# A graph layer's setup, reordered: the first two groups' picks beside the key table, the rest of the table in later steps

## The chip, the cores and the metric

The kernel runs on one core of a Trainium2 chip. A core has five engines that run their own instruction queues in order: TensorE (PE, matrix products into PSUM), VectorE (DVE), ScalarE (ACT), GpSimd (POOL) and SyncE (SP), which here only issues DMAs. The metric is the device time of one execution in microseconds (us). Times of the kernel before: a median of 1493.0 us over three runs, 1492.52 to 1494.01.

## The reference

A message-passing layer with 6250 nodes of 64 features and 200000 edges sorted by target node, followed by a residual and a normalisation:

```
w   = silu(edge_attr_32 @ W1 + b1) @ W2 + b2            # (E, 9)
msg = einsum('ef,em,fmg->eg', x[src], edge_attr_9 * w, W_tp)
agg = segment_sum(msg, dst) / sqrt(16)
gamma, beta = split(silu(node_vec[:, None] @ Wn1 + bn1) @ Wn2 + bn2, 2)
out = layernorm(x + agg * (1 + gamma) + beta)
```

## The kernel before, in words

**Groups and steps.** The edges are cut into tiles of 128 and these into 98 groups of 16 tiles (`KB`). `setup` prepares constants and the first groups; then a loop of 98 steps runs, and step i finishes the window products of group i, the weights of group i + 1 and the first layer of group i + 2.

**Rows of x.** Each tile needs the 128 rows `x[src]`. They come in three ways. Most tiles are gathered by an indirect DMA that POOL issues (L99, one a tile), up to `AHEAD` = 6 groups ahead, into seven buffers `hs`; a buffer comes free after the window product (L533) of its group. The last `picked(g)` tiles of a group, four, or three in every fifth group, are not gathered but picked by TensorE (`pick`, L488): a tile's one-hot matrix `hot_k` (seven blocks, `hots`, L481, on VectorE) is multiplied by all of x, which stands in SBUF as a high and a low part (`xs`, 14 matmuls of 448 columns, L500) and VectorE selects one of seven columns per row and adds up (L509, L511). In every fourth group from 7 on, one tile's rows are loaded one by one by SP (L115, 32 in a step).

**The key table.** `hots` compares a key per edge. `keys_of` (L204, ten VectorE operations) makes from `src` a key and a remainder `jl` for each picked edge. `keys_first` (L225) spreads the keys of groups 0 and 1 with a diagonal (L232) and a product with ones (L233). For all other groups `keys_rest` (L235) transposes the key table in three blocks (L239), copies them on ScalarE (L241) and stores them to the DRAM table `kd`; `load_keys` (L414) reads it back to all partitions as `kr`, and `keys` (L476) copies it to PSUM for each group.

**Weights and windows.** `hidden` (L424) and `second` (L442) are the two layers of the edge network. `weights` (L452) turns their result and multiplies it by the edge's nine coefficients and by `oh`, the one-hot of the edge's target relative to its tile's first node (`near`, L404), which needs the node differences `rel = dst - row`. `windows` (L519) sums the rows by target in PSUM, `project` applies W_tp, `place` and `bring` put windows at their nodes, `finish` normalises.

**Setup's order.** The order in the text is the order on each engine (a manual schedule). `split` (L245) makes the high and low part of x, one seventh at a time, as ScalarE copies and VectorE subtracts. Then come the picks of group 0, both layers, the whole remaining key table (L277), the transposes of small tables (`p_row`, `p_f`, `p_cn`, `p_nid`), all differences `rel` (L327, 1536 columns), and the loop with step 0, in which group 1 is picked. PSUM tags that matter: `px` has two buffers (picks), `s` one (`second`, and in setup pk of group 1), `r` one (keys), `pz` two (windows), `p1` one. `SPG` are the groups with rows by SP.

Of the kernel before, what the change touches and what calls it, by code (L numbers as in the profile page):

```python
# [7 lines left out]
F32 = mybir.dt.float32  # L8
I32 = mybir.dt.int32
# [7 lines left out]
P = 128  # L17
N, F, M, D, H, E = 6250, 64, 9, 32, 64, 200000
NJ = 49
# [48 lines left out]
def gnn_resnorm_kernel(ctx: ExitStack, tc: tile.TileContext, x, src, dst, dst_row, ea, sh, cn,  # L68
# [18 lines left out]
    with ExitStack() as fast:  # L87
# [58 lines left out]

        def setup(temp):
# [12 lines left out]
            row_i = xb.rearrange("p j f -> p (j f)")[:, 0:NBLK * KB].bitcast(I32)  # L160
            load(0, split=True)
            nc.sync.dma_start(dst_i[:, 0:2 * KB], dst[:, 0:2 * KB])
            nc.sync.dma_start(row_i[:, 0:2 * KB], rows(dst[0, 0:2 * KB], P))
# [5 lines left out]
            for c in range(KB // 4):  # L169
                q = c * D  # L170
                nc.sync.dma_start(b2c[q:q + 2 * M, :], bass.AP(tensor=b2.tensor, offset=b2.offset,
                                                               ap=[[0, 2], [1, M], [1, 1]]))
            first_i = temp.tile([NBLK, KB], I32)
            nc.sync.dma_start(first_i, dst[0].rearrange("(g k) -> g k", k=KB))
            cn_j = temp.tile([NJ, P], F32)
            nc.sync.dma_start(cn_j, cn)

# [4 lines left out]
            sel_i = temp.tile([KB, P], I32)  # L182
# [5 lines left out]
            for g in range(AHEAD):  # L188
                gather(g)

# [6 lines left out]
            nc.vector.tensor_copy(li, n_i[:, 0:J])  # L197
            ones = temp.tile([P, P], F32)
            nc.vector.memset(ones, 1.0)


            zt_r = ztw

            def keys_of(g0, g1):  # L204

                c0, c1 = g0 * Q, g1 * Q
                s_f, kp, kh, rest, t0, t1 = [zt_r[:, k * C + c0:k * C + c1] for k in range(6)]
                ti = [t.bitcast(I32) for t in (t0, t1)]
                g2 = min(g1, NBLK - 1)
                nc.vector.tensor_copy(s_f[:, 0:(g2 - g0) * Q].rearrange("p (g k) -> p g k", k=Q),  # L210
                                      src_i.rearrange("p (g k) -> p g k", k=KB)[:, g0:g2, KB - Q:])
                if g1 == NBLK:
                    nc.vector.tensor_copy(s_f[:, (g2 - g0) * Q:], src_i[:, NT - Q:NT])
                nc.vector.tensor_scalar(ti[0], s_f, 2675.0, None, op0=ALU.mult)
                nc.vector.tensor_scalar(ti[0], ti[0], 17, None, op0=ALU.logical_shift_right)
                nc.vector.tensor_copy(kp, ti[0])
                nc.vector.scalar_tensor_tensor(rest, kp, -float(J * J), s_f, op0=ALU.mult, op1=ALU.add)
                nc.vector.tensor_scalar(ti[1], rest, 37.0, None, op0=ALU.mult)
                nc.vector.tensor_scalar(ti[1], ti[1], 8, None, op0=ALU.logical_shift_right)
                nc.vector.tensor_scalar(kh, ti[1], float(P), None, op0=ALU.mult)  # L220
                nc.vector.tensor_add(s_f, kp, kh)
                nc.vector.scalar_tensor_tensor(jl[:, c0:c1], kh, -float(J) / P, rest, op0=ALU.mult, op1=ALU.add)
                return s_f

            def keys_first(g, kf, tag):  # L225

                pk_t[g] = psum.tile([P, Q, P], F32, tag=tag, name=f"pk{g}")
                for t in range(picked(g)):
                    c = (g + 1) * Q - picked(g) + t
                    d0 = NBLK * KB + c * P  # L230
                    dg = xb.rearrange("p j f -> p (j f)")[:, d0:d0 + P]
                    nc.vector.tensor_scalar(dg, ident, kf[:, c:c + 1], None, op0=ALU.mult)  # L232
                    nc.tensor.matmul(pk_t[g][:, t, :], ones, dg, start=True, stop=True)  # L233

            def keys_rest(kf):  # L235
                for c0 in range(LB * Q, C, P):
                    n = min(P, C - c0)
                    p_kt = psum.tile([P, P], F32, tag="r", name=f"p_kt{c0}")
                    nc.tensor.transpose(p_kt[0:n], kf[:, c0 - LB * Q:c0 - LB * Q + n], ident)  # L239
                    kt = zt_r[:, 6 * C + c0 // 2:6 * C + c0 // 2 + P // 2].bitcast(F16)  # L240
                    nc.scalar.copy(kt[0:n], p_kt[0:n])  # L241
                    nc.sync.dma_start(kd[c0:c0 + n, :], kt[0:n])


            def split(h):  # L245
                xh = gam[:, h * J:(h + 1) * J, :].rearrange("p l f -> p f l")
                nc.scalar.copy(xs[0][:, h], xh)
                nc.vector.tensor_sub(xs[1][:, h], xh, xs[0][:, h].bitcast(F32))

            kf = keys_of(0, LB)  # L250
            keys_first(0, kf, "r")
            hots(0, 0, 1)
            for h in range(J):
                split(h)
                if h == J // 2:
                    hots(0, 1, 2)
            one = temp.tile([1, 1], F32)
            nc.vector.memset(one, 0.0)
            nc.scalar.activation(one, one, AF.Silu)
            pick(0, 0)  # L260
            hots(0, 2, Q)
            hidden(0)
            keys_first(1, kf, "s")
            hots(1, 0, 1)
            nc.vector.tensor_copy(wi, n_i[:, 0:W])
            nc.vector.tensor_sub(rel[:, 0:2 * KB], dst_i[:, 0:2 * KB], row_i[:, 0:2 * KB])
            near(0)
            pick(0, 1)
            hots(1, 1, Q)
            second(0)  # L270
            pick(0, 2, [[lambda: None, lambda: None], weights(0)])
            hidden(1)

            nc.sync.dma_start(dst_i[:, 2 * KB:], dst[:, 2 * KB:])
            nc.sync.dma_start(row_i[:, 2 * KB:], rows(dst[0, 2 * KB:], P))
            load(LB)
            keys_rest(keys_of(LB, NBLK))  # L277
            load_keys(LB)
            for q in range(2):
                n = (M + 1 - q) // 2  # L280
                nc.sync.dma_start(wtc2[q * F:(q + 1) * F, 0:n, :], wtp[:, q:M:2, :])
            nc.vector.memset(wtc2[F:P, 4], 0.0)
            zero = temp.tile([P, 1], F32)
            nc.vector.memset(zero, 0.0)
            nc.scalar.copy(zt[F:P, :, 4].rearrange("p a k w -> p a (k w)"),
                           zero[F:P, :, None].to_broadcast([F, 4, KW]))
            nc.sync.dma_start(wn1c, wn1.rearrange("o h -> h o"))
            nc.sync.dma_start(bn1c, bn1.unsqueeze(1))
            nc.sync.dma_start(wn2a[0:H, :], wn2)
            nc.sync.dma_start(wn2a[H:H + 1, :], bn2.unsqueeze(0))  # L290
            row_f = temp.tile([P, len(SPG)], F32)
            nc.vector.tensor_scalar(row_f, src_i[:, SPG[0] * KB:NBLK * KB:SPS * KB], 4.0 * F, None, op0=ALU.mult)
            p_row = psum.tile([len(SPG), P], F32, tag="s", name="p_row")
            nc.tensor.transpose(p_row, row_f, ident)
            nc.vector.tensor_copy(row_a, p_row)
            first_t = temp.tile([NBLK, KB], F32)
            nc.scalar.copy(first_t, first_i)
            p_f = psum.tile([KB, NBLK], F32, tag="s", name="p_f")
            nc.tensor.matmul(p_f, first_t, ident[0:NBLK, 0:NBLK], start=True, stop=True)
            nc.scalar.copy(first_f, p_f)  # L300
            p_cn = psum.tile([P, NJ], F32, tag="r", name="p_cn")
            nc.tensor.matmul(p_cn, cn_j, ident[0:NJ, 0:NJ], start=True, stop=True)
            cn_s = temp.tile([P, NJ], F32)
            nc.scalar.copy(cn_s, p_cn)
            nc.sync.dma_start(cn_d, cn_s)
            gate_load(0)

            nc.vector.tensor_copy(lo, lo_i)
            sel_a = temp.tile([KB, P], F32)
            nc.vector.tensor_scalar(sel_a, sel_i, -0.5, None, op0=ALU.is_gt)  # L310
            sel = temp.tile([KB, P], F32)
            nc.vector.scalar_tensor_tensor(sel, sel_i, W - 0.5, sel_a, op0=ALU.is_lt, op1=ALU.mult)
# [6 lines left out]
            p_nid = psum.tile([P, NBLK], F32, tag="s", name="p_nid")  # L319
            nc.tensor.matmul(p_nid, sel, first_f, start=True, stop=True)  # L320
            nc.vector.scalar_tensor_tensor(nid, p_nid, pw, lo, op0=ALU.add, op1=ALU.subtract)
            nc.vector.tensor_add(ident2, ident[:, 0:F], ident[:, F:P])
            for k in range(2):
                nc.vector.memset(ht[k][H:H + 1], 1.0)
            nc.vector.memset(eps, EPS)

            nc.vector.tensor_sub(rel[:, 2 * KB:], dst_i[:, 2 * KB:], row_i[:, 2 * KB:])  # L327
            nc.vector.memset(rel[:, NT:], 0.0)
            if E % P:
                nc.vector.memset(rel[E % P:, NT - 1:NT], 0.0)  # L330
# [579 lines left out]
```

## Time and profile before

| what | us |
|---|---|
| median of the timed runs | 1493.0 |
| profiled execution | 2388.1 |
| its span | 2386.3 |
| PE busy | 1675.3 (70%) |
| DVE busy | 1206.6 (51%) |
| ACT busy | 521.1 (22%) |
| POOL busy, nearly all in 1168 gathers | 1109.7 (47%) |
| L500, 5208 pick matmuls, busy | 1304.3 |
| PE's first matmul of pick(2,0) begins | 148.7 |

The profiled execution is much longer than a timed one, so its durations of single instructions are of more use than its sum. In the timeline a line gives start, duration, engine, source line, operation and, in brackets, the idle time before it and what ended that; "remote" means that no releaser was found, "issue" that the engine waited for nothing that the profile shows. Ends of matmuls are modelled.

### The profile page before, as it was taken

To read this page: it belongs to the slowest core of one execution; us is meant where nothing else is said; L and a number is where in the kernel's file an instruction comes from. 1 tells how busy PE (TensorE), PEld (TensorE's weight loads), DVE (VectorE), ACT (ScalarE), POOL (GpSimd) and SP (SyncE) were. 2 spreads that over 40 slices of the span, in tenths; PEclk is the share of its full clock that TensorE was granted. 3 is DMA by queue.
4 is the path that set the end of the run, shared out by engine and by line. 5 is a ranking of instruction groups with operands and counts; after the bars stand their busy time and mean duration, and the time that the engine had idled before them with its cause. 6 is when DMAs were issued, how large, how long until landed. Compare 5 with 4: busy or idle time off the path is not lost. (4 is left out here: it accounts for less than half of the span.)

```text
span 2386.3 us, 34188 instructions
## 1 busy us (share of the span) xinstructions
PE 1675.3 (70%) x10858; PEld 1367.1 (57%) x10858; DVE 1206.6 (51%) x2157; ACT 521.1 (22%) x1326; POOL 1109.7 (47%) x1177
## 2 busy tenths in 40 slices
PE   3076777676776767677767677677777676877797
PEld 2065656564655655556656556565656564656586
DVE  3154545454545454545555545454545454545476
ACT  1021212121212121211222222121212121212133
POOL 7644444444444545444545454545444544444410
PEclk7598888888888988887888898788887888888898
DMA  3121111111111111111111111111111111111110
GB/s 114 34 62 40 47 34 41 36 46 37 38 35 42 41 39 38 44 37 38 35 36 44 38 37 45 35 36 35 47 34 37 36 45 35 37 35 46 33 38 5
DMA packets 90264, 96.13 MB, mean 40 GB/s; under 512 B 36744, under 2 KB 51290, under 8 KB 90074
## 3 DMA queue, kind: packets, MB, share of 16 engines
q1 hardware_dynamic: 52122, 53.89, 7.9%
q0 software_dynamic: 37376, 38.35, 7.1%
q8 instruction: 89, 1.46, 0.2%
q10 hardware_dynamic: 576, 1.61, 0.2%
q14 instruction: 101, 0.83, 0.1%
HBM read 92.01 MB, written 1.73 MB: 39 GB/s over the span
## 5 line engine op out<-in xcount | busy, mean ns | idle before, releaser
L99 POOL DMA_INDIRECT hs<-in_x_dram,src_i x1168 | 1108.4, 949 | 1167.6 <-PE pz L533 825.8
L500 PE MATMUL px<-xs_w,hot_k 128*128 128x448 f32 x5208 | 1304.3, 406 | 432.3 <-DVE xm L509 377.0
L500 PEld LDWEIGHTS px<-xs_w,hot_k 128*128 128x128 f32 x5208 | 1067.0, 213 | 567.4 <-DVE xm L509 409.5
L509 DVE SCALAR_TENSOR_TENSOR xm<-li,jl,px 128x448 f32<-128x448 f32 x372 | 251.8, 677 | 936.4 <-remote 698.0
L485 DVE TENSOR_TENSOR hot_k<-pk,nk 128x896 fp32r<-128x896 f32 x372 | 387.7, 1081 | 2.8 <-PE pk L233 2.8
L511 DVE TENSOR_REDUCE hs<-xm 128x64 f32<-128x448 f32 x372 | 230.6, 620 | 12.9
L438 ACT ACTIVATE st<-p,b1c 128x1024 f32<-128x1024 f32 x98 | 109.2, 1115 | 542.4 <-PE p L429 365.3
L543 ACT COPY ztw<-pz 64x140 f32<-64x140 f32 (+1 forms) x780 | 209.2, 268 | 21.7 <-PE pz L533 10.3
L447 PE MATMUL p<-st,w2p 128*32 128x256 f32 x784 | 71.8, 430 | 152.4 <-DVE xb L370 102.9
L601 ACT COPY carry<-ps 128x128 f32<-128x128 f32 x48 | 12.8, 266 | 649.4 <-PE ps L595 587.0
L533 PEld LDWEIGHTS pz<-a,hs 128*64 128x64 f32 x3116 | 116.5, 155 | 58.7 <-issue 55.1
L447 PEld LDWEIGHTS p<-st,w2p 128*32 128x32 f32 x784 | 17.6, 113 | 228.7 <-issue 127.1
L533 PE MATMUL pz<-a,hs 128*64 128x63 f32 x3116 | 131.7, 244 | 11.7 <-issue 11.5
L467 DVE TENSOR_TENSOR a<-oh,p 128x1008 f32<-128x1008 f32 x98 | 117.9, 1203 | 3.3
L429 PE MATMUL p<-ea,w1bd 64*128 64x512 f32 x392 | 111.5, 642 | 0.7 <-issue 0.7
L728 ACT ACTIVATE var<-var,eps 128x2 f32<-128x2 f32 (+1 forms) x25 | 7.4, 295 | 374.6 <-DVE var L725 374.6
L579 PE MATMUL pt<-ztw,wtc 128*64 128x112 f32 x960 | 71.9, 308 | 18.6 <-ACT st L438 18.6
L579 PEld LDWEIGHTS pt<-ztw,wtc 128*64 128x64 f32 x960 | 61.7, 170 | 20.6 <-ACT st L438 20.3
L554 DVE TENSOR_TENSOR r<-pt,r 112x128 fp32r<-112x128 f32 x48 | 13.9, 289 | 97.2 <-issue 86.2
L479 ACT CAST pk<-kr 128x512 f32<-128x512 f16 (+1 forms) x96 | 54.6, 569 | 16.5 <-DVE hot_k L485 11.1
L450 ACT ACTIVATE p2s<-p,b2c 128x256 f32<-128x256 f32 x98 | 45.9, 468 | 48.6 <-issue 30.5
L457 DVE STREAM_TRANSPOSE p<-p2s 128x256 f32<-128x256 f32 x98 | 44.1, 450 | 14.9 <-issue 14.4
(138 smaller groups left out, 552.7 us busy)
## 6 DMA issues: line engine op xcount, KB each, us to landing
hs<-in_x_dram SPq DMA_DIRECT2D x2944, 0.2 KB
ea<-in_ea_dram SPq DMA_DIRECT2D x48, 512.0 KB
hs<-in_x_dram,src_i POOLq DMA_INDIRECT x1168
kr<-kd SPq DMA_DIRECT2D x48, 256.0 KB
sh<-in_sh_dram SPq DMA_DIRECT2D x49, 144.0 KB
cb<-cn_d SPq DMA_DIRECT2D x12, 128.0 KB
out_dram<-o SPq DMA_DIRECT2D x24, 64.0 KB
dst_i<-in_dst_dram SPq DMA_DIRECT2D x1, 768.0 KB
```

What stands on the lines that cost most here:

```text
L99: hs_dma[g] = [nc.gpsimd.indirect_dma_start(out=hs[g][:, t - g * KB, :], out_offset=None, in_=x, in_offset=bass.IndirectOffsetOnAxis(ap=sr ...
L429: nc.tensor.matmul(p1[:, i, :].rearrange("p (c t e) -> p c t e", c=4, t=4), w1bd[i * 64:(i + 1) * 64, :], e[i * 64:(i + 1) * 64, :].rearra ...
L438: nc.scalar.activation(st[g], p1_t.pop(g), AF.Silu, bias=b1c)
L447: nc.tensor.matmul(p2[g][c * D:(c + 1) * D, 0, :].rearrange("p (i e) -> p i e", i=2), w2p, s[:, :, c * P:(c + 1) * P], start=True, stop=True)
L467: nc.vector.tensor_mul(a[g], oh_t.pop(g)[:, :, None, :].to_broadcast([P, KB, M, W]), sw.unsqueeze(3).to_broadcast([P, KB, M, W]))
L485: nc.vector.tensor_tensor(hot_k[g, t], pk_t[g][:, t, None, :].to_broadcast([P, J, P]), nk.unsqueeze(2).to_broadcast([P, J, P]), op=ALU.is_ ...
L500: nc.tensor.matmul(px.rearrange("p f l -> p (f l)"), hot_k[g, t][:, h, :], xs[i][:, h].rearrange("p f l -> p (f l)"), start=(h == 0 and i ...
L509: nc.vector.scalar_tensor_tensor(xm, li[:, None, :].to_broadcast([P, F, J]), jl[:, c:c + 1], px, op0=ALU.is_equal, op1=ALU.mult)
L511: nc.vector.tensor_reduce(hs[g][:, tiles(g) - q + t, :], xm, AX.X, ALU.add)
L533: mm = nc.tensor.matmul(pz[v][v * F:(v + 1) * F, k // 2].rearrange("p m w -> p (m w)"), hsg[:, k0 + k, :], ag[:, k0 + k].rearrange("p m w ...
L543: nc.scalar.copy(z[h * F:(h + 1) * F, 0:5 - h, k0 + v:k0 + n:2, :].rearrange("p m k w -> p k m w"), pz[v][v * F:(v + 1) * F, 0:(n + 1 - v) ...
L579: nc.tensor.matmul(pt[h * F:(h + 1) * F, 0, 0:KW], wtc2[:, c, :], z[h][:, c], start=(c == 0), stop=(c == 4))
```

## The change

In the setup:

- `split` reads x in order and writes with a stride; before it read with a stride and wrote in order.
- `keys_of` becomes a list of ten functions on given buffers; setup runs it for groups 0 and 1 and for the next 32 groups (`KC`) alone. The other two thirds are made in steps 2 and 4, between picks, and transposed and stored at the ends of steps 3 and 5 (`keys_turn`).
- The keys of group 1 are spread by TensorE between the matmuls of pick(0,0), into tag `r`; those of group 0 into tag `pz`. Tag `s` is no longer used for them.
- Step 0 of the loop becomes part of the setup: gather(6), the picks of group 1, `hidden(2)`, `second(1)`, `windows(0)`, `weights(1)`. The loop starts at step 1. The small tables' transposes and copies stand between these picks.
- `rel` is made for 2 groups, then up to group 10 in setup, and the rest in four pieces in step 6. The rows it subtracts lie in a part of `gam` (`row_r`) instead of `xb`.
- DMAs of SP: small tables, W_tp and the second load of edge data go ahead of the large `dst` and `row` loads; the 32-column loads of `dst` and `row` go behind the bias loads. The two rows of ones in `ht` are copied by ScalarE instead of set by VectorE.

The diff, cut:

```diff
+        def keys_of(g0, g1, buf):
...
+            return [
+                take,
+                lambda: nc.vector.tensor_scalar(ti[0], s_f, 2675.0, None, op0=ALU.mult),
...
+                lambda: nc.vector.scalar_tensor_tensor(jl[:, c0:c1], kh, -float(J) / P, rest,
+                                                       op0=ALU.mult, op1=ALU.add)]
+
+        def keys_turn(g0, kf, tag, kt):
+            c0 = g0 * Q
+            p_kt = psum.tile([P, P], F32, tag=tag, name=f"p_kt{g0}", bufs=1 + (tag == "pz"))
+            nc.tensor.transpose(p_kt, kf, ident)
+            nc.scalar.copy(kt, p_kt)
+            stores.append(lambda: nc.sync.dma_start(kd[c0:c0 + P, :], kt))
+
+        def relative(k0, k1):
+            nc.vector.tensor_sub(rel[:, k0:k1], dst_i[:, k0:k1], row_r[:, k0:k1])
...
             def split(h):
-                xh = gam[:, h * J:(h + 1) * J, :].rearrange("p l f -> p f l")
-                nc.scalar.copy(xs[0][:, h], xh)
-                nc.vector.tensor_sub(xs[1][:, h], xh, xs[0][:, h].bitcast(F32))
+                xh = gam[:, h * J:(h + 1) * J, :]
+                hi, lo_ = [xs[i][:, h].rearrange("p f l -> p l f") for i in range(2)]
+                nc.scalar.copy(hi, xh)
+                nc.vector.tensor_sub(lo_, xh, hi.bitcast(F32))
...
+            for f in keys_of(0, LB, kb):
+                f()
+            for f in keys_first(0, kb[0], "pz"):
+                f()
+            spread = keys_first(1, kb[0], "r")
...
+            hots(0, 0, 1)
+            for h in range(J):
+                split(h)
...
+            hots(0, 1, 2)
+            pick(0, 0, [spread[0:4], [lambda: hidden(0)]])
+            hots(0, 2, Q)
...
+            pick(0, 1)
+            second(0)
+            hots(1, 0, 1)
...
+            kb = [ztw[:, k * P:(k + 1) * P] for k in range(6)]
+            for f in keys_of(LB, LB + KC, kb):
+                f()
+            pick(0, 2)
+            hidden(1, act=False)
+            kt = temp.tile([P, P], F16)
+            keys_turn(LB, kb[0], "pz", kt)
+            hidden_act(1)
+            while stores:
+                stores.pop(0)()
+            load_keys(LB)
...
+            nc.tensor.transpose(p_row, row_f, ident)
+            hots(1, 1, 2)
+            pick(1, 0)
+            nc.vector.tensor_copy(row_a, p_row)
+            nc.vector.tensor_sub(rel[:, 0:2 * KB], dst_i[:, 0:2 * KB], row_i)
+            near(0)
...
+            for f in weights(0):
+                f()
...
+            hots(1, 2, 3)
+            pick(1, 1)
...
+            windows(0)
+            second(1)
+            hots(1, 3, Q)
+            keys(2)
...
+            pick(1, 2)
+            hidden(2)
+            hots(2, 0, 1)
+            for f in weights(1):
+                f()
+            hots(2, 1, 2)
+            pick(1, 3)
+            relative(2 * KB, KN)
+            near(2)
+            hots(2, 2, Q)
...
-            setup(temp)
-
-            for i in range(NBLK):
+            kb, kt = setup(temp)
+            more_of = {2: keys_of(LB + KC, LB + 2 * KC, kb), 4: keys_of(LB + 2 * KC, NBLK, kb),
+                       6: [lambda k=k: relative(KN + k, min(KN + k + 352, NBLK * KB))
+                           for k in range(0, NBLK * KB - KN, 352)]}
+
+            for i in range(1, NBLK):
...
-                for t in range(2, Q):
-                    pick(i + 1, t)
+                beside = more_of.pop(i, [])
+                n = -(-len(beside) // (Q - 1))
+                for t in range(2, Q + 1):
+                    for f in beside[(t - 2) * n:(t - 1) * n]:
+                        f()
+                    if t < Q:
+                        pick(i + 1, t)
+                if i in (3, 5):
+                    keys_turn(LB + KC * (i - 1) // 2, kb[0], "s", kt)
```

## The prediction

> **What bounds the kernel now.** The page comes first: the profiled execution took 2388.1 us (span 2386.3) where the timed runs have a median of 1493.0. Something in it is 895 us that a timed run does not have, so I look for what waits. The table of waits (engine, line waited for, total, times, longest):
>
> ```profile
> POOL hs L99 <- PE pz L533: 825.8, 90, 14.8
> DVE xm L509 <- remote: 698.0, 119, 36.4
> ```
>
> POOL waits for TensorE to free a gather buffer; VectorE waits for a pick that by TensorE's own record is long over. The timeline of the setup shows it at its worst:
>
> ```profile
> 35.32 1.08 PE L447 MATMUL p<-st,w2p 128*32 128x256 f32 x8 [12.44 <-issue]
> 36.33 5.16 PE L500 MATMUL px<-xs_w,hot_k 128*128 128x448 f32 x14
> 41.42 1.13 PE L429 MATMUL p<-ea,w1bd 64*128 64x512 f32 x4
> ...
> 88.18 0.68 DVE L509 SCALAR_TENSOR_TENSOR xm<-li,jl,px 128x448 f32<-128x448 f32 x1 [36.45 <-remote]
> ...
> 93.80 0.55 DVE L222 SCALAR_TENSOR_TENSOR jl<-ztw 128x384 f32<-128x384 f32 x1
> ```
>
> The pick ends at 41.5, its reader starts at 88.18. The windows view (span, busy us of PE, PEld, DVE, ACT, POOL, granted clock, DMA share, GB/s) compares setup, first step and the stretch after the last gather:
>
> ```profile
> 60.00:118.00 58.00, 2.77 (x9) 1.27 (x9) 7.49 (x24) 2.91 (x7) 40.65 (x43) 0.50 0.15 34
> 118.00:149.00 31.00, 24.29 (x171) 19.09 (x172) 19.87 (x31) 8.57 (x24) 13.34 (x14) 0.92 0.37 80
> 2270.00:2372.00 102.00, 97.98 (x746) 82.77 (x746) 77.49 (x140) 34.49 (x91) 6.12 (x7) 1.00 0.08 23
> ```
>
> Without gathers PE is 96% busy at full clock and the late completions are gone. I take the late completions for a cost of recording, since 1493 us has no room for them, and read the timed bound from two clean rates.
>
> TensorE: four whole steps at the end,
>
> ```profile
> 2281.29 1.13 PE L429 MATMUL p<-ea,w1bd 64*128 64x512 f32 x4
> 2340.06 1.13 PE L429 MATMUL p<-ea,w1bd 64*128 64x512 f32 x4
> ```
>
> 58.77 us with 15 picks, so 14.7 a step. Four average steps have 15.2 picks; a pick is 14 x 0.205 = 2.87 (56 matmuls in 11.47 us), which makes 14.8. One 1.6 us wait inside that sample may not be typical (14.4), and early steps carry a gate product of 0.4 (15.2). POOL:
>
> ```profile
> 24.34 0.95 POOL L99 DMA_INDIRECT hs<-in_x_dram,src_i  x1 [0.30 <-issue]
> 127.77 1.84 POOL L99 DMA_INDIRECT hs<-in_x_dram,src_i  x1 [14.31 <-PE pz L533]
> ```
>
> 1168 gathers at 0.95 + 0.30 = 1.25 (1.254 with the few long ones) are 1465 us in one queue, 14.9 a step. From the first at 4.0, with 2 for landing (estimate), the 14.7 from the last group's window product (2371.6) to the end and 1.8 around the span: a floor of 1487. The two streams are within 1% of each other; which one ends last decides how much of a shorter setup is kept.
>
> **The Trainium skill.** "Perfetto Trace Analysis", per-instruction lifecycle: a matmul's recorded end is an estimate, and its semaphore follows later; the 47 us above agree that the record can't be trusted for completion. "TensorE: Matmul & The Clock Gate", part 1: an idle array falls to half clock. The trace agrees: clock 0.50 in 60 to 118, a matmul of 5.16/14 = 0.37 against 0.205. "SBUF — State Buffer", who interferes with whom: VectorE with two SBUF inputs blocks a GpSimd reader. The gathers at 9.15 and 10.73, beside L248, took 1.28 and 1.40 instead of 0.95. "DMA: Bandwidth & Descriptors", anatomy of one DMA: some 2 us fixed; the records of before have no landing times.
>
> **Before's setup without late completions.** I go along the program order with the durations of the trace. Up to px(0,0) it is as recorded: 16.3. VectorE: product and reduce 0.68 + 0.62, hots(0,2) 1.08, four diagonals 0.86, to 19.4; pk(1) by 20.1, recorded hots(1,0) to 22.0, near(0) to 22.6; px(0,1) is done at 22.9, so its 1.3 run to 24.3 and hots(1,1) to (1,3), 3.1, to 27.4. Only then is the PSUM tag s free for second(0): PE 0.8, px(0,2) 2.8, to 31.1. weights(0), 2.2 after p2s, ends at 31.3, product and reduce 32.6. The whole table, ten operations, 4.9 (89.44 to 94.35): 37.5. Three transposes through one PSUM buffer, 0.5 + 0.3 each, to 39.6; stores, 2 us by the DMA page, kr near 44. p_row, p_f, p_cn and p_nid with their copies: PE free at 42.3. pick(1,0) 2.8 and hidden(2) 1.2: 46.5, second(1) and windows(0) 1.9: 48.4. Picks (1,1), (1,2): 54.0. pick(1,3) waits for xm(1,1), which on VectorE stands behind rel (1.76), near, hots(2,0..3) (4.3), xm(1,0) and weights(1): 54.9. PE starts pick(2,0) at **57.7**.
>
> **After's setup.** Three diagonals, then four more and the pw chain (1.8 in all) fill the wait for pk(0): hots(0,0) to 9.3. Seven splits read in order and write with a stride, before the reverse. No row shows this: bounds 0.56 (what the table's two-input operations of 384 columns took) and 1.86 (twice L248's 0.93); I take 0.87 apart as now, to 15.4. hots(0,1) to 16.4, px(0,1) to 19.2; hidden(0) and pk(1) sit in gaps of px(0,0). second(0) no longer waits for tag s: 19.9; px(0,2) 22.7; hidden(1) 23.9. VectorE meanwhile: xm(0,0), hots(0,2), xm(0,1), hots(1,0), to 21.6, row_f and the first third of the table, ten operations of 128 columns. Between their 8-column sum, 1.82, and their 384-column sum, 4.65, that is 2.7: 24.4. The transpose, which stands ahead of pick(1,0) in PE's queue, then p_row: 25.1. px(1,0) 27.9. VectorE: xm(0,2), hots(1,1), xm(1,0) to 29.2, row_a 29.5, rel, near, weights(0), hots(1,2) to 33.5. p_cn needs p_row's buffer (29.5): px(1,1) 30.0 to 32.8; p_nid, windows(0) whose second half waits for nid (35.3), second(1): 36.5. px(1,2), hidden(2), px(1,3): 43.5, where pick(2,0) starts. **Gain 14.2 us** on PE.
>
> **What rides along, at nothing.** SP: the small tables and load(2) go ahead of dst; these eight issues, 0.3 to 1.4 each as recorded, end near 21, and the 32-column dst and row parts, issued by 16, are wanted at 29. The kd store waits for kt at 25, kr is back near 29.5, and ScalarE asks for it after windows(0), at 36; if it were late by more than 6, keys(2) and hidden_act(2) behind it, and then second(2), would wait. gather(6) is in the same place of POOL's queue, seven buffers free. sel_i grows to 128 partitions beside POOL's 2 us wait for src_i. ScalarE's two ht copies replace two 0.49 memsets.
>
> **What comes back later.** Steps 2 and 4: ten VectorE operations each (2.7), and after steps 3 and 5 a transpose on PE (0.5), a copy and a store. Step 6: four differences of 352 columns; L327's slope, (1.755 - 0.184)/1504, gives 0.52 each, 2.1. And VectorE enters step 1 late: hots(2,3) ends about 49.1, 5.6 after PE starts. It works 1206.6/98 = 12.3 a step, so 2.5 of 14.8 is spare. I put 1 for the transposes with their wait for tag s, 0.6 for step 1, 1.6 of the 7.5 for overflow in 2, 4 and 6: **3.2 back**. The kd rows of the later thirds are read from step 31 on. Net 11.0, so 1482.0. Against the profiled execution's 2388.1 the same 11 us; its late completions can shift by more than that.
>
> **Cases and rivals.** 0.2% (3 us) is what a measurement here can tell.
> 1. TensorE's stream ends last: from 57.7, 94 steps of 14.8, one pick and the 46.2 behind hidden(97) give 1500, 1462 to 1537 with 14.4 to 15.2. Then the gain is kept: 1482, own range 1477 to 1487. Chance 0.45. For it: before lies 6 above POOL's floor, and the floor falls if recording lengthened the gathers.
> 2. PE sets the end now, but POOL's floor stops the gain: 1487 to 1490. Chance 0.17.
> 3. The gathers already set the end: PE starts 25 us late but catches up. No POOL instruction goes away, so no change, 1490 to 1496. For it: 1487 against 1493. Against it: it needs PE's steps well under 14.9. Chance 0.20.
> 4. Slower: VectorE becomes the bound from the setup to step 6. If none of its spare time is usable, its 5.6 delay, 5.4 of table and 2.1 of rel reach PE, 13.1; splits of 1.86 add 0.99 x 7 = 6.9. 20.0 less 14.2 makes 1499. It decides once these exceed 14.2. Chance 0.18.
>
> Cases 1 and 2 are faster (0.62), 3 is the same, 4 slower. I predict 1482; the range 1476 to 1498 reaches over all cases and leaves out a better case 1 and the worse part of 4.
>
> **What would show it.** After: table operations of about 0.27 in the setup; second(0) no longer behind hots(1,3); TensorE busy far more in 16 to 60 (12.55 us of 44 now), though late completions may move. Split rows above 0.93, or xm waiting behind table operations in steps 2, 4, 6, would speak for case 4. Case 3 would show as fewer POOL waits for PE and the same median. Wrong would be, above all, my reading of the late completions: if part of them occurs in timed runs, setup's 118 us is partly real, and the gain could be several times larger.

## The result, and the profile after

The kernel after takes 1495.7 us (median of 20 runs, 1492.7 to 1498.0), the kernel before beside it 1493.3 (20 runs, 1492.0 to 1495.5): a ratio of 1.0014, 95% interval 1.0008 to 1.002. The change gains nothing: after is 2.4 us slower, where 11 us less were predicted. The profiled execution of after took 1494.0, so unlike before's it shows what a timed run does. One thing is needed to read what follows: in some series of runs every execution of every kernel, before's too, takes about 2400 us instead of 1493, so each ratio below is to the kernel before in the same series.

The head of the page of after (PEld is TensorE's loading of weights):

```profile
span 1492.2 us, 34211 instructions
...
PE 1437.1 (96%) x10858; PEld 1204.9 (81%) x10858; DVE 1205.2 (81%) x2179; ACT 516.7 (35%) x1328; POOL 1110.8 (74%) x1177
```

PE was busy 70% of before's long profile and is busy 96% here. The waits of after (engine, line waited for, total, times, longest) that answer to the two shown of before:

```profile
POOL hs L99 <- issue: 321.7, 1055, 0.3
DVE xm L545 <- PE px L536: 203.3, 161, 2.6
```

The 826 us for which POOL waited for TensorE are gone. What is left is the 0.3 us between gathers: POOL runs from 4.1 to 1469.5 without waiting for anybody. And VectorE waits for picks at most 2.6 us, with TensorE named, where it had waited 36 for "remote". None of this is the work of the change: e8 below, a kernel with before's setup profiled in a series of 1493 us, has TensorE busy 97%, POOL standing no more than the 0.3 us between gathers, and 2.6 us as the longest wait for a pick. The windows view of after (span, busy us of PE, PEld, DVE, ACT, POOL, clock, DMA share, GB/s):

```profile
16.00:60.00 44.00, 36.44 (x235) 28.45 (x234) 34.54 (x66) 14.72 (x35) 33.24 (x36) 0.92 0.57 145
60.00:118.00 58.00, 56.60 (x438) 47.27 (x436) 47.86 (x93) 17.34 (x50) 43.76 (x47) 1.00 0.24 51
118.00:150.00 32.00, 29.98 (x229) 25.03 (x228) 26.95 (x55) 11.67 (x29) 24.34 (x26) 1.00 0.26 63
```

TensorE's granted clock is 0.92 in the setup and 1.00 in the mean of the two later stretches. Its timeline in the setup (start, duration, engine, line, operation):

```profile
19.96 0.64 PE L483 MATMUL p<-st,w2p 128*32 128x256 f32 x8
...
39.69 6.03 PE L536 MATMUL px<-xs_w,hot_k 128*128 128x448 f32 x28
...
47.28 1.15 PE L569 MATMUL pz<-a,hs 128*64 128x63 f32 x32
54.23 2.10 PE L609 MATMUL pr<-wtc,ztw 128*112 128x64 f32 x10 [5.80 <-issue]
```

second(0) begins at 19.96; the 28 matmuls at 39.69 are the picks (1,3) and (2,0), so pick(2,0) starts near 42.7. VectorE's timeline shows the first third of the table:

```profile
22.41 0.22 DVE L155 CAST ztw<-src_i 128x128 f32<-128x128 int32 x1
...
24.77 0.28 DVE L170 SCALAR_TENSOR_TENSOR jl<-ztw 128x128 f32<-128x128 f32 x1
```

So the setup did what it was to do. POOL's timeline shows what I had not expected there, and the end of the queue:

```profile
8.02 0.94 POOL L99 DMA_INDIRECT hs<-in_x_dram,src_i  x1 [0.30 <-issue]
9.26 1.51 POOL L99 DMA_INDIRECT hs<-in_x_dram,src_i  x1 [0.30 <-issue]
11.08 5.10 POOL L99 DMA_INDIRECT hs<-in_x_dram,src_i  x1 [0.30 <-issue]
...
1468.59 0.94 POOL L99 DMA_INDIRECT hs<-in_x_dram,src_i  x1 [0.30 <-DMA hs<-in_x_dram,src_i]
```

Two gathers beside the seven subtractions of the split take 1.51 and 5.10 us; over the first 20 us the queue loses 4.9 us against its 1.25 a gather. In before's profile it lost 1.6. This is called the loss in the split below.

### The profile page after: what moved, and what is told of

Same layout as the page of the kernel before. It is cut to its first block, busy times and chain, and to the rows that moved or that the text cites. A ratio compares the mean times of both kernels' runs of the same rounds, so it can differ in the third digit from the quotient of the medians.

```text
span 1492.2 us, 34211 instructions
## 1 busy us (share of the span) xinstructions
PE 1437.1 (96%) x10858; PEld 1204.9 (81%) x10858; DVE 1205.2 (81%) x2179; ACT 516.7 (35%) x1328; POOL 1110.8 (74%) x1177
## 4 chain that ended last, share of the span: by engine, by line
PE 73%; POOL 10%; DVE 5%; issue 5%; DMA 4%; ACT 2%; SPq 1%; POOLq 0%; DVEq 0%; ACTq 0%
PE px L536 55%; POOL hs L99 10%; PE pz L569 6%; PE p L465 4%; DMA hs<-in_x_dram,src_i 3%; PE pt L615 3%; PE p L483 3%; DVE xm L545 1%; SPq L115 1%; PE ps L631 1%; ACT st L474 1%; DVE hot_k L521 1%; DVE hs L547 1%; PE ps L661 1%; ACT L474 1%
## 5 line engine op out<-in xcount | busy, mean ns | idle before, releaser
L536 PE MATMUL px<-xs_w,hot_k 128*128 128x448 f32 x5208 | 1117.4, 369 | 1.5 <-DVE hot_k L521 1.4
L536 PEld LDWEIGHTS px<-xs_w,hot_k 128*128 128x128 f32 x5208 | 954.5, 189 | 79.2 <-DVE xm L545 2.1
L569 PEld LDWEIGHTS pz<-a,hs 128*64 128x64 f32 x3116 | 100.0, 138 | 55.1 <-issue 48.5
L569 PE MATMUL pz<-a,hs 128*64 128x63 f32 x3116 | 113.2, 225 | 14.5 <-issue 4.5
L483 PE MATMUL p<-st,w2p 128*32 128x256 f32 x784 | 62.6, 391 | 8.2 <-DVE xb L406 8.2
L615 PE MATMUL pt<-ztw,wtc 128*64 128x112 f32 x960 | 55.3, 261 | 2.7 <-ACT st L474 2.2
L465 PEld LDWEIGHTS p<-ea,w1bd 64*128 64x128 f32 x392 | 29.5, 185 | 31.6 <-issue 23.8
L497 DVE TENSOR_TENSOR p<-p,sh 128x72 f32<-128x72 f32 x196 | 47.3, 241 | 6.7
L615 PEld LDWEIGHTS pt<-ztw,wtc 128*64 128x64 f32 x960 | 47.0, 137 | 4.4 <-ACT st L474 3.3
```

The costliest lines, as they stand in the source:

```text
L465: nc.tensor.matmul(p1[:, i, :].rearrange("p (c t e) -> p c t e", c=4, t=4), w1bd[i * 64:(i + 1) * 64, :], e[i * 64:(i + 1) * 64, :].rearra ...
L483: nc.tensor.matmul(p2[g][c * D:(c + 1) * D, 0, :].rearrange("p (i e) -> p i e", i=2), w2p, s[:, :, c * P:(c + 1) * P], start=True, stop=True)
L536: nc.tensor.matmul(px.rearrange("p f l -> p (f l)"), hot_k[g, t][:, h, :], xs[i][:, h].rearrange("p f l -> p (f l)"), start=(h == 0 and i ...
L569: mm = nc.tensor.matmul(pz[v][v * F:(v + 1) * F, k // 2].rearrange("p m w -> p (m w)"), hsg[:, k0 + k, :], ag[:, k0 + k].rearrange("p m w ...
L615: nc.tensor.matmul(pt[h * F:(h + 1) * F, 0, 0:KW], wtc2[:, c, :], z[h][:, c], start=(c == 0), stop=(c == 4))
```

## The experiments

Two theories, called G and D in the first expectations. **Gathers** (G): TensorE's stream did become shorter, but the gather queue, which nothing shortened, catches up with it and sets the end. **TensorE** (D): the gain is lost to TensorE's own later work. A third that was alive at first: the **split's new orientation** (strided writes) blocks the gathers and costs the time.

### The split, and fewer gathers: e1 to e4

e1 is the kernel after with before's orientation of the split, e2 the kernel before with the new one. In e3 (of after) and e4 (of before) every third group gathers one tile less, 33 in all; that tile is filled with rows 0 to 127 by one plain transfer, so these two compute other values there, as do e5, e6, e14, e16 and e17 below.

```diff
 e1, against after
-                xh = gam[:, h * J:(h + 1) * J, :]
-                hi, lo_ = [xs[i][:, h].rearrange("p f l -> p l f") for i in range(2)]
+                xh = gam[:, h * J:(h + 1) * J, :].rearrange("p l f -> p f l")
 e3 and e4, in gather(g)
-                for t in range(g * KB + (g in SPG), g * KB + tiles(g) - picked(g))]
+                for t in range(g * KB + (g in SPG), g * KB + tiles(g) - picked(g) - (g % 3 == 0))]
+            if g % 3 == 0:
+                k = tiles(g) - picked(g) - 1
+                hs_dma[g].append(nc.sync.dma_start(hs[g][:, k, :], x[0:P, :]))
```

> The changed kernel with the split of before (reads with a stride, writes in order). Theory G: the gathers set the end, and the changed split holds them up by 3.3 us (one gather of 5.10 us). Then the loss of the first 20 us of gathers falls from 4.9 to about 1.6 us and the time from 1495.7 to 1492.5 (1491.5 to 1493.5). Theory D: TensorE sets the end, and the work put into steps 2 to 6 gives back what the setup gains. Then nothing moves: 1495.7. If the seven subtractions in a row, and not the stride, block the gather, the long gather stays and so does 1495.7.

> The kernel before with the changed split alone (reads in order, writes with a stride). Theory G: one or two gathers beside the subtractions take 3 to 5 us, the stream of gathers ends 2 to 4 us later and so does the kernel: 1495 to 1497. Theory D: 1493.3, since nothing waits for the gathers at the end. If only seven subtractions without a break block a gather, the order of before, with a one-hot between them, loses less: under 1 us, 1493.3 to 1494.

> The changed kernel, with one gather in every third group (33 of 1168) replaced by a plain load of the first 128 rows of x by SP; these tiles get other rows, so this part of the computation is changed. POOL has 33 x 1.25 = 41 us less to do. Theory G: TensorE's stream alone is left, 13 us below the gathers' by the slack in the trace: 1482 (1479 to 1486). Theory D: the gathers don't matter, 1495.7.

> The same 33 replaced gathers in the kernel before. Theory G with the setup's gain real: TensorE of before starts group 2 some 11 to 14 us later than the changed one, so 1490 to 1494, and the gap to the changed kernel with the same edit is 8 to 14 us. Theory D, no net gain of TensorE: both edited kernels within 3 us of each other. A third reading, in which the setup of before was no later without recording, also gives equal times, but both near 1482.

This series ran at 2401 (before, 43 runs). e1: 2409.1, ratio 1.0025 (1.0006 to 1.0045). e2: 2405.1, 1.0019 (0.9998 to 1.0041). e3: 2369.3, 0.9863 (0.9835 to 0.9892). e4: 2361.4, 0.9836 (0.9802 to 0.987). In these long executions fewer gathers help both kernels alike, so they say nothing on which stream ends a 1493 us run. One reading is good in any series, though. POOL's timeline of e1:

```profile
9.31 6.86 POOL L99 DMA_INDIRECT hs<-in_x_dram,src_i  x1 [0.30 <-issue]
```

With before's orientation back, a gather takes even longer: the new orientation is not needed for the long gather. In e2, where it is all that is new, two gathers take 2.42 and 3.43 us and the loss is 4.6.

### Fewer gathers at 1493 us, and other places for the picks: e5 to e8

e5 and e6 are e3 and e4 again. e7 (of after) and e8 (of before) move the groups with three picks from 0, 5, 10, ..., 95 to 0, 6, 11, ..., 96, which takes one gather from group 95, near the end, and gives it to group 96; the result is the same.

```diff
-    return Q - (g % 5 == 0)
+    return Q - (g == 0 or g > 1 and g % 5 == 1)
```

> The same kernel as e3 (changed kernel, 33 gathers replaced by a plain load of 128 rows, which changes that part of the computation), again because the chip of the first four runs needed 2401 us for the kernel before. Where before takes 1493: theory G (gathers set the end) 1482 (1479 to 1486), theory D (TensorE and the late work set it) 1495.7. Where before takes 2400: about 41 us less than the changed kernel, as in e3.

> The same kernel as e4 (before, 33 gathers replaced). Where before takes 1493: theory G with a real gain in the setup 1490 to 1494, so 8 to 14 us above e5; if before is held by its gathers by more than a few us, lower, and the gap to e5 is the net gain of TensorE. Theory D: e5 within 3 us of this one. Where before takes 2400: about 2361, as in e4.

> The changed kernel with the groups of three picks moved from 0, 5, 10, ... 95 to 0, 6, 11, ... 96: as many picks and gathers, the result unchanged, but one gather of group 95 becomes one of group 96, and one pick after the window product of group 95 falls away. Theory G: the end is the gathers of group 95, 2.2 us and 44.2 us of TensorE behind them, so 1.25 + 2.87 = 4.1 us less: 1491.6 (1490.5 to 1493). Theory D: no change, 1495.7. Where before takes 2400: no clear change.

> The kernel before with the same move of the groups of three picks. If its gathers alone set its end: 1493.3 less 4.1, 1489.2. If TensorE's late start sets it: 1493.3. In between if both end together. Where before takes 2400: no clear change.

Before: 1493.3 (41 runs). e5: 1486.2, ratio 0.9956 (0.9942 to 0.9969). e6: 1493.9, 1.0004 (0.9996 to 1.0013). e7: 1494.2, 1.0008 (0.9999 to 1.0016). e8: 1493.6, 1.0002 (0.9996 to 1.0009).

So 33 gathers fewer are worth nothing to the kernel before and 9.5 us to the kernel after: before is set by TensorE, after is not. e6 therefore shows before's TensorE stream undisturbed, and e5 that of after. I take, from the three timelines, the start of each group's window product and list how far it is ahead of e6's:

| group | 1 | 2 | 4 | 6 | 16 | 40 | 76 | 80 | 88 | 92 | 95 |
|---|---|---|---|---|---|---|---|---|---|---|---|
| e6, start | 66.2 | 83.2 | 113.2 | 140.5 | 290.1 | 646.6 | 1173.7 | 1231.0 | 1348.4 | 1405.9 | 1447.3 |
| after ahead by | 18.9 | 12.4 | 10.6 | 9.3 | 9.4 | 9.4 | 9.4 | 7.4 | 3.5 | 0.4 | -0.7 |
| e5 ahead by | 19.3 | 13.0 | 11.3 | 9.9 | 10.2 | 10.5 | 10.9 | 10.9 | 10.8 | 11.0 | 11.0 |
| after: start of its product behind the end of the group's last gather | 7.3 | 15.9 | 17.8 | 15.1 | 15.7 | 13.0 | 2.6 | 1.7 | 4.1 | 4.8 | 2.2 |

This is the whole case in one table. After keeps some 9 us through 70 steps and loses them between groups 76 and 92, where its product starts 2 to 5 us after the end of its group's last gather. e5, the same kernel with the gathers out of reach, keeps 11 to the end. (In time e5 and e6 differ by 7.7, in their profiled spans, 1481.2 and 1492.9, by 11.7; the runs of e5 spread over 5.5.) The windows view of after and of e5 between 1100 and 1440:

```profile
1100.00:1440.00 340.00, 329.89 (x2505) 276.39 (x2505) 270.27 (x455) 116.71 (x303) 257.04 (x273) 1.00 0.26 59
```

```profile
1100.00:1440.00 340.00, 338.55 (x2598) 283.11 (x2597) 277.32 (x472) 121.14 (x315) 249.91 (x264) 1.00 0.26 60
```

TensorE idles 10.1 us of this stretch in after and 1.5 in e5. Where it idles, the timeline of after shows, at the window product (L569):

```profile
1298.80 1.15 PE L569 MATMUL pz<-a,hs 128*64 128x63 f32 x32 [2.19 <-DMA hs<-in_x_dram,src_i]
...
1374.62 1.15 PE L569 MATMUL pz<-a,hs 128*64 128x63 f32 x32 [2.94 <-issue]
...
1447.97 1.15 PE L569 MATMUL pz<-a,hs 128*64 128x63 f32 x32 [1.05 <-DMA out_dram<-o]
```

Six such waits of over 1 us from 1148 on add up to 9.3; the first of these three names the gather, others are put down to something else that ended near the same moment. e5 has none at this line. e7 confirms no more than the direction: 1.6 of the 4 us hoped for and an interval that overlaps that of after. Its queue had caught up by group 76 already (1.6 us ahead of the product) and lost more in the split (6.2 us, with a gather of 6.95).

### hots(0,1) between the subtractions: e9 and e13

Before breaks the row of seven subtractions after the fourth with a one-hot block. The same kernel was run twice.

```diff
             for h in range(J):
                 split(h)
+                if h == J // 2:
+                    hots(0, 1, 2)
...
-            hots(0, 1, 2)
```

> The kernel after, with hots(0,1) back in the middle of the seven splits, as in the kernel before. Gathers theory (the gather queue sets the end of the kernel after from about step 76 on, and lost 4.9 us in the first 20 us beside the unbroken row of subtractions against 1.6 before): the row is broken, the long gather falls from 5 us to 2 to 3, the loss to about 2, and the time by 2 to 3 us, to 1493. TensorE theory (the 10 us are lost to TensorE's own later work): no change or 1 us more, 1496 to 1497, since the loss of the gathers costs nothing. On a chip where completions come late: within 0.3% of before by both.

> The same kernel as the run with hots(0,1) in the middle of the splits, for a chip on which the kernel before takes 1493. Gathers theory (the gather queue sets the end of the kernel after from about step 76 on): the row of subtractions is broken, the gathers lose 2 us instead of 4.9 in the first 20 us, and the time falls by 2 to 3 us from 1495.7 to 1493 (ratio 0.9998). TensorE theory (the gain is lost to TensorE's own later work): 1495.7 to 1497, whatever the gathers lose. If the row's length is not what blocks the gather, the loss stays near 5 and this run says nothing on the time.

Both fell into long series: 2407.8 against 2400.6, 1.0034 (1.0015 to 1.0054), and 2435.8 against 2426.2, 1.0027 (1.0003 to 1.0051). The trace answers the part on the loss: 5.9 and 4.6 us in the first 20. Breaking the row only splits the long gather into two (4.11 and 3.40 in e9). My expectation fell.

### More rows by SP: e10 to e12

A version that might beat both: SP, which loads one tile row by row in every fourth group, takes more tiles from POOL. e10 loads 26 instead of 23 (37 rows a step), e11 is e10 with e9's edit, e12 is 31 tiles (43 rows) with e9's edit.

```diff
 e10
-SPG = range(7, NBLK, SPS)
+SPG = sorted([*range(7, NBLK, 7), *range(10, NBLK, 7)])
...
 e12
-SPS = 4
+SPS = 3
-SPR = P // SPS
+SPR = -(-P // SPS)
...
```

> The kernel after with 26 instead of 23 tiles loaded row by row by SP (groups 7, 10, 14, 17, ...: 37 rows a step instead of 32), so 3 gathers fewer, with the same result. Gathers theory: 3 x 1.25 = 3.8 us less, 1492. TensorE theory: no change, 1495.7. If SP becomes late (37 rows x 0.33 = 12.2 us, with its loads 13.5 to 14 of a step of 14.95): window products wait for SP's rows and the time rises above 1496.

> Both edits together: hots(0,1) in the middle of the splits, and 26 tiles by SP. Gathers theory: both gains add, 6 to 7 us less than after: 1489 (ratio 0.997), faster than the kernel before by 4. TensorE theory: 1496. If SP becomes late: above e9.

> hots(0,1) in the middle of the splits, and a tile by SP in every third group: 31 tiles, 8 gathers fewer than after, 43 rows in a step. Gathers theory: 8 x 1.25 + 2.5 = 12.5 us of room, but TensorE's own stream (1486.2 in the kernel with 33 gathers fewer) then ends last: 1486 to 1488, ratio 0.9955. SP's 43 rows take 43 x 0.33 = 14.2 us and its loads 1 to 2 of a step of 14.95: if SP cannot keep up, each step is lengthened by up to 1 us and the time passes 1500, up to 1550. TensorE theory: 1496.

In a series with before at 2400.6 they took 2790.0 (1.1636, 1.1589 to 1.1683), 2787.2 (1.1615, 1.1569 to 1.1661) and 3001.7 (1.2513, 1.2465 to 1.2561). SP became late. Its queue in e12 (timeline: start, time, line, transfers), and in after:

```profile
1024.99 24.05 SPq L116 DMA_DIRECT2D hs<-in_x_dram  x42
...
1055.48 22.92 SPq L116 DMA_DIRECT2D hs<-in_x_dram  x43
```

```profile
1007.30 10.83 SPq L115 DMA_DIRECT2D hs<-in_x_dram  x32
...
1020.86 10.28 SPq L115 DMA_DIRECT2D hs<-in_x_dram  x32
```

In e12 one round of SP takes 30.5 us, and 98 steps of 30.6 are its 3002: SP sets the step. In the waits of e12, TensorE stands behind it through the edge data that SP issues after its rows:

```profile
PEld p L467 <- DMA ea<-in_ea_dram: 588.5, 46, 25.1
```

In after's run of 1494 us, 32 rows take 10.3 to 10.8 us and the load of their addresses 2.2, of a step of 15. There 37 rows at 0.33, which need two address loads, would take 16 to 17 us and be too many as well; that is an estimate, and no 1493 us series has seen these kernels.

### Four gathers fewer: e14, e16 and e17

This edit asks what one gather is worth at the end. Groups 12, 24, 36 and 48 gather one tile less; in all four the product starts over 13 us after the group's last gather, so TensorE does not wait for them there.

```diff
-                for t in range(g * KB + (g in SPG), g * KB + tiles(g) - picked(g))]
+                for t in range(g * KB + (g in SPG), g * KB + tiles(g) - picked(g) - (g in (12, 24, 36, 48)))]
...
```

> The kernel after with one gather less in groups 12, 24, 36 and 48 (the tile gets rows 0 to 127 of x by one plain transfer, so the result changes). All four lie before step 76, where TensorE still had 15 us of slack. Gathers theory: the time falls one for one with the gathers' time, 4 x 1.25 = 5.0 us, to 1490.7 (ratio 0.9983); 33 fewer gave only 9.5 us, since TensorE then ends last at 1486.2. TensorE theory: 33 fewer gained 9.5 us by 0.29 a gather, so 4 fewer give 1.2, 1494.6.

> The kernel after with one gather less in groups 12, 24, 36 and 48, once more, for a chip on which the kernel before takes 1493. Gathers theory: 4 x 1.25 = 5.0 us less than after, 1490.7 (ratio 0.9983). TensorE theory: 4 x 0.29 = 1.2 us less, 1494.6 (ratio 1.0008). On a chip where it takes 2400: within 0.3% of before, and nothing told apart.

> The kernel after with one gather less in groups 12, 24, 36 and 48, a third time, for a chip on which the kernel before takes 1493. Gathers theory: 4 x 1.25 = 5.0 us less than after, 1490.7 (ratio 0.9983). TensorE theory: 4 x 0.29 = 1.2 us less, 1494.6 (ratio 1.0008). On a chip where it takes 2400: within 0.3% of before, and nothing told apart.

e14 and e16 met long series, 2424.4 against 2426.2 (0.999, 0.997 to 1.0011) and 2400.7 against 2398.5 (1.0004, 0.998 to 1.0027), and tell nothing. e17: **1490.4** against 1493.9, 0.9977 (0.9966 to 0.9987). The gathers theory said 1490.7, the other 1494.6. Four gathers of 1.25 us, taken out between 190 and 740 us, come off the end one for one: 5.3 us below after's 1495.7, where 5.0 were taken out, and the interval lies clear of after's. The loss in the split is 4.8 in e17, as in after. The timeline of e17 shows what is left of the late waits, two instead of six, and its windows view the idle time between 1100 and 1440, 5.6 instead of 10.1:

```profile
1294.18 1.15 PE L572 MATMUL pz<-a,hs 128*64 128x63 f32 x32 [1.91 <-ACT p2s L489]
...
1370.14 1.15 PE L572 MATMUL pz<-a,hs 128*64 128x63 f32 x32 [1.79 <-DMA hs<-in_x_dram,src_i]
```

```profile
1100.00:1440.00 340.00, 334.41 (x2528) 279.86 (x2527) 272.71 (x463) 116.39 (x303) 257.30 (x272) 1.00 0.25 59
```

### Candidates with the full result: e15 and e18

e15 is e9 with four picks instead of three in groups 30 and 60. e18 has the whole split as before, orientation and place of hots(0,1), and four picks in group 30.

```diff
 e15
-    return Q - (g % 5 == 0)
+    return Q - (g % 5 == 0 and g not in (30, 60))
 e18
+    return Q - (g % 5 == 0 and g != 30)
```

> hots(0,1) in the middle of the splits, and groups 30 and 60 with four picked tiles instead of three, so two gathers fewer and two picks more, with the same result. Gathers theory: the gathers' end moves 2.5 + 2.9 us ahead, to 1490.3, and TensorE's own stream from 1486.2 to 1486.2 + 2 x 2.9 = 1492; the later one sets the time, 1491 to 1492.5, faster than before by 1 to 2. TensorE theory: two picks more on the bound, 1495.7 + 5.7 = 1501.

> The kernel after with the whole split as in the kernel before (its orientation, and hots(0,1) in the middle), and four picked tiles in group 30 instead of three (one gather less, one pick more), with the same result. The gathers' loss in the first 20 us, seen in the trace on any chip: 1.6 to 3 us if both parts of the old split together are what kept it small, near 5 or 6 if something else in the new setup blocks them. On a chip where the kernel before takes 1493: gathers end 1.25 + 2 to 3.2 us earlier, 1491 to 1492.5, and TensorE's stream at 1486.2 + 2.9 = 1489 stays below it; with a loss near 5, 1494.5. On a chip where it takes 2400: within 0.3% of before.

Both fell into long series: 2435.4 against 2426.2 (1.0023, 0.9999 to 1.0048) and 2412.1 against 2398.8 (1.0049, 1.0027 to 1.0071). Whether either beats before at 1493 us stays open; no faster version with the full result was found. POOL's timeline of e18 settles one point:

```profile
9.30 3.92 POOL L99 DMA_INDIRECT hs<-in_x_dram,src_i  x1 [0.30 <-issue]
13.52 3.21 POOL L99 DMA_INDIRECT hs<-in_x_dram,src_i  x1 [0.30 <-issue]
```

A loss of 5.5 us with VectorE's row as in before. So to put back the orientation, the place of hots(0,1) or both does not bring the small loss back. All traced kernels with the new setup lose 4.6 to 6.2; of four profiles of before's setup with its own split three lose 1.6 and one (e4) 3.1, and with the new orientation (e2) 4.6. Nor do ScalarE's copies beside the row decide it: they pause for 1.9 us in before, which loses 1.6, and for 2.0 in e3, which loses 6.1. What makes the loss larger in the new setup is not found.

## Why the prediction was wrong

**The setup's gain was larger than I walked, and more of it came back.** "Gain 14.2 us": at the window product of group 1, e6 against after, it is 18.9. After's walk was right (pick(2,0) at 43.5, measured 42.7; second(0) at 19.9, measured 19.96; table operations of 0.27, measured 0.22 to 0.29). Before's was 4.1 short: pick(2,0) starts near 61.8 in e6, not at 57.7. The timeline of e6 shows where:

```profile
45.59 4.94 PE L503 MATMUL px<-xs_w,hot_k 128*128 128x448 f32 x14
...
66.20 1.15 PE L536 MATMUL pz<-a,hs 128*64 128x63 f32 x32
68.55 1.17 PE L576 MATMUL pr<-wtc,ztw 128*112 128x64 f32 x10 [1.20 <-issue]
```

pick(1,0) begins 3.3 later than I had it and takes 4.94, not 2.8, with waits inside. "3.2 back": it was 9.6, 18.9 to 9.3 by group 6. I gave step 1 0.6 us; it cost 6.5. Most of it is project(0), which stands 5.8 us in after (54.23, above) against 1.2 in e6. It writes PSUM tag r, which holds group 3's keys until VectorE, late as predicted, has made hots(3): the last of these ends at 54.13 in after and at 68.45 in e6, and in both project(0) begins 0.10 later. The profile names no releaser, so this is read from the times and the program. Most of the rest is TensorE's clock after that wait, in the windows view of after:

```profile
54.00:56.00 2.00, 1.77 (x10) 1.80 (x10) 0.13 (x1) 0.00 (x0) 1.69 (x2) 0.50 0.19 33
```

The granted clock is 0.50 up to 58, and the ten matmuls of project(0) take 2.10 us, where e6, at 1.00, needs 1.17. I had looked at what VectorE's lateness does to picks and not at whom its PSUM buffers hold up. Groups 2 to 6 cost 3.1 (2.6 predicted with the transposes), of which 2.3 are waits for edge data that SP issues, which I had at nothing. That the net came out near, 11.0 predicted, 9.3 in after and 11.0 at the end of e5, is luck: 4.7 too little gain and 6.4 too little given back.

**The step that failed is the floor of the gathers.** I wrote "a floor of 1487", counting 14.7 us behind the window product of the last group. But the last group is not the one that binds. In after the product of group 95 starts 2.2 us after the end of its last gather, and 44.2 us of TensorE stand behind it (1447.97 to 1492.2); the last gathers of groups 96 and 97 end over 7 us ahead of the products that need them. Before's profile had shown this tail, 44.6 us:

```profile
2341.69 1.15 PE L533 MATMUL pz<-a,hs 128*64 128x63 f32 x32
```

Done rightly: 4.0 + 1149 gathers up to group 95 x 1.2505 (1436.8, measured in after) + 1.6 lost in the split + 2 for landing + 44.6 + 1.8 around the span = 1490.8. That is 2.5 below the kernel before (1.5 with the tail of 45.6 in e6), so a setup that leaves the gathers as they were could gain no more than that. The new setup also cost the gathers 3.3 us more in the split: 1494.1, against 1494.0 for the profiled execution; the median lies 1.7 above that, which stays unexplained. So case 2 happened, "POOL's floor stops the gain", at a floor that I had 7 too low, about half of it the tail and half the split. Case 3 had the right time for the wrong reason (the gathers did not set the end before; e6). Case 1 had the right bound of before; its sum of 1500 was too high because it took 14.8 a step, where e6 needs 14.7 (66.2 to 1447.3 in 94 steps). Case 4 did not come (VectorE's delay was paid in step 1 and was over by group 6).

**The steady 1.25 a gather was right, the price of the split was not.** The Trainium skill, "SBUF — State Buffer", who interferes with whom, says that VectorE with two SBUF inputs blocks a GpSimd reader. I read its size from before's 1.28 and 1.40 and put nothing in the sum for the new setup. The trace agrees that such rows and gathers collide and shows a far larger size, 5.10 and up to 6.95 us for one gather, several subtractions long; since POOL waits for nothing else, each us there is a us at the end once the gathers set it. That these subtractions are what holds the gathers is read from their times; no run here has the gathers without them.

**"The late completions for a cost of recording" was wrong.** In long series the timed executions take 2400 too, and after's recorded one took 1494. The 47 us between a pick's recorded end and its reader belong to such a series as well; the longest such wait in after is 2.6. Nothing was lost by it in the number, since the sums were made from 1493.

## What to carry to other kernels

When two streams end within 1% of each other, shortening one is worth at most the distance to the other's floor; that floor is the latest end over all items of the second stream, each taken with the work that must follow it, and the last item need not be the one that gives it. A list of how far one kernel is ahead of the other, group by group, shows at once whether a gain was never made, was paid back, or was caught by another queue. And a cause is best weighed by removing a little of it far from the end, where it can act only through the queue itself.

## What was not expected of the hardware

- Whole series of runs take 2400 us for a kernel that takes 1493 in others; it is not tied to one chip, as one chip gave both (1493.3 in one series, 2426.2 in another). In the profile of before, of that kind, SP needs 19.24 us for 32 row transfers that take 10.3 to 10.8 in after, and TensorE's results reach VectorE up to 36 us late while gathers run. The cause is open.
- One indirect gather can take 5 to 7 us beside a row of VectorE subtractions that each read two SBUF operands, where others beside a like row take 1.3 to 1.5. What decides between the two is open.
- The strided split that I had bounded between 0.56 and 1.86 takes 1.00 us an operation, against 0.93 with the read strided.
